# Values and keys by seven products: another order of the products, and one PSUM tile of two banks for two of them

## The chip, the cores and the metric

The kernel runs on one core of a Trainium2 chip. The metric is the time of one execution on the device, in microseconds (us), as the median of several runs. All values are float32.

## The reference

Sixteen samples of x, each 1024 nodes by 256 channels, go through two layers; only the first is touched here.

```
h   = max(layernorm(x), 0)                       # per sample, 1024 x 256
A   = 2 * | |sigmoid(difference of column means) - 0.5| - 0.5 |
g   = relu((h.T @ (adj * A)) * para)             # queries, 256 x 1024
k,v = halves of h @ kv_w                         # kv_w is 256 x 512
x   = x + softmax(q k.T * scale) v               # 4 heads of 64
# second layer, for every sample, with batch norm over all samples:
h1  = max(layernorm(x), 0)
x   = x + bn(relu(bn((A_hat @ h1) @ W1.T)) @ W2.T)
```

## The kernel before

**Order of the work.** The order of instructions on each engine is written out by hand; the program's waits are then set by the tile framework from what each instruction reads and writes. A tile is the unit of this tracking, and a tile taken from a pool waits until all readers of the tile that had its place are through. For each sample b the kernel runs `attention(b)` (scores, exponentials, weighted values), then `graph_seven(b + 1)`, which makes queries, keys and values of the next sample, then `linear1_all(b)`, the first matrix products of layer two for the sample just finished. Sample 0 and sample 1 get their keys and values from the plainer `graph`; samples 2 to 15, 14 in all, from `graph_seven`. The change lies in the second half of `graph_seven`.

**Seven products.** Keys and values are block products with 2 x 2 blocks, done by a scheme with seven products in place of eight. The class `Seven` holds one such product; `V` makes values (turned, so that nodes lie on partitions) and `K` makes keys. `product(m)` issues product m on TensorE: for `K` one matmul of 128 x 512 (line 713), for `V` four matmuls of 128 x 128 (line 718). In the profile each float32 matmul shows as two records. Products 1, 6, 5 and 3 are added up in one PSUM tile, the running sum "x"; after each of 1, 6, 5 and 3 ScalarE copies the present sum out (`copy`, line 728), and the next of them may not be added before the copy is done. Products 2, 7 and 4 have PSUM places of their own and are added by VectorE to what was copied (`add`, line 731): 2 once, 7 twice, 4 once.

**PSUM.** The kernel uses eight banks, each a place of 128 x 512 float32. The pool `ps_s` has three slots of two banks, `ps_o` and `ps_t` one bank each. `ps_s` also holds the score tiles of attention, the tiles `gps[0]` and `gps[1]` of the graph product, and the sums of `linear1` (line 1027). Before the change `product` takes a tile for itself when it needs one: both running sums, values' fourth and keys' seventh from `ps_s` (one of a slot's two banks is then used), values' seventh and keys' fourth from `ps_o`, both seconds from `ps_t`.

**What stands around it.** Just before, TensorE ends the graph product in `f_gpsx` (in `ps_t`) and `f_gps7` (in `ps_o`). ScalarE copies `f_gpsx` (line 656); VectorE adds `gps[1]` (line 658), the block sums `kt1` to `kt4` (lines 663 to 667), `f_gps7` (line 668) and `gps[0]` (line 670). Then, between the products, VectorE's queue holds, in this order: `V.add(0, 0, 2)`, two multiplications that make the queries (line 740), `add1` (line 938, which adds the attention's result to x), the statistics `norm.stats(0, 4)` and `norm.invert(0, 4)` (lines 253 to 259; GpSimd makes the power, line 260), `V.add(1, 0, 7)` and `V.add(1, 1, 7)`, a shift (line 266), `norm.stats(4, NC)` and `norm.invert(4, NC)`, and `V.add(1, 0, 4)`. `norm.relu` on ScalarE (line 281) makes h of layer two, which `linear1` multiplies; its second half, `norm.relu(4, NC)`, stands behind `K.copy(0, 1)` on ScalarE. The DMAs of the stretch (`leave`, `arrive`, `load_more`) are issued between `add1` and the statistics.

Of the kernel before, what the change touches and what calls it, by code (L numbers as in the profile page):

```python
# [10 lines left out]
F32 = mybir.dt.float32  # L11
# [6 lines left out]
P = 128  # L18
# [11 lines left out]
def fast_path(  # L30
# [141 lines left out]
    ps_o = ctx.enter_context(tc.tile_pool(name="fps_o", bufs=1, space=PSUM))  # L172
    ps_t = ctx.enter_context(tc.tile_pool(name="fps_t", bufs=1, space=PSUM))


    with ExitStack() as stage:
        ps_s = stage.enter_context(tc.tile_pool(name="fps_s", bufs=3, space=PSUM))
# [20 lines left out]
        for c in range(NC):  # L198
            if LASTING[c] is None:
                t = big.tile([P, N], F32, tag=f"adj{c}", name=f"f_adj_{c}")  # L200
            else:
                t = lasting.tile(
                    [P, N], F32, tag=LASTING[c], name=f"f_adj_{c}", bufs=4 if c < 4 else 1
                )
# [304 lines left out]
        def graph_seven(b, left, norm, load_more, last):  # L509
# [16 lines left out]
            for d in range(CC):  # L526
                t = pp.tile([P, N], F32, tag="p", name=f"f_hT_{b}_{d}")
# [38 lines left out]
            x = ps_t.tile([P, 512], F32, tag="t", name=f"f_gpsx_{b}")  # L566
# [44 lines left out]
            sums = big.tile([P, 2, 4, P], F32, tag="row", name=f"f_kvs_{b}")  # L611
# [62 lines left out]
            def relu_queries(d):  # L674

                nc.scalar.activation(qT[:, d, :], qT[:, d, :], AF.Relu, scale=-SCALE)

            class Seven:


                def __init__(self, name, n, c, turned):
                    self.name, self.n, self.c, self.turned, self.ps = name, n, c, turned, {}
                    sums, o = (ps_s, "s"), (ps_o, "o")
                    self.banks = {
                        "x": sums,
                        2: (ps_t, "t"),
                        7: o if turned else sums,
                        4: sums if turned else o,
                    }

                def place(self, key, pool, tag):
                    ps = pool.tile([P, 512], F32, tag=tag, name=f"f_{self.name}ps{key}_{b}")
                    self.ps[key] = ps.rearrange("p (n q) -> p n q", n=4) if self.turned else ps

                def product(self, m):
                    w = lambda i, k: kvw_t[:, k, ts(2 * self.n + i, P)]
                    s = lambda q: sums[:, self.n, q]
                    left, right = {
                        1: (w(0, 0), part(0, 0)),
                        2: (w(0, 1), part(1, 0)),  # L700
                        3: (s(3), part(1, 1)),
                        4: (w(1, 1), kt4),
                        5: (s(0), kt1),
                        6: (s(1), kt2),
                        7: (s(2), kt3),
                    }[m]
                    more = m in (3, 5, 6)
                    key = "x" if more or m == 1 else m
                    if not more:
                        self.place(key, *self.banks[key])  # L710
                    ps = self.ps[key]
                    if not self.turned:
                        nc.tensor.matmul(  # L713
                            ps, left, right, start=not more, stop=True, skip_group_check=more
                        )
                        return
                    for n in range(4):
                        nc.tensor.matmul(  # L718
                            ps[:, n],
                            right[:, ts(n, P)],  # L720
                            left,
                            start=not more and n == 0,
                            stop=n == 3,
                            skip_group_check=True,
                        )
# [6 lines left out]

            V = Seven("v", 1, lambda i, j: v[:, 4 * j : 4 * j + 4, ts(i, P)], True)
            K = Seven("k", 0, lambda i, j: kT[:, i, ts(j, 512)], False)
            V.product(1)
            V.copy(0, 0)
            V.product(2)
            V.add(0, 0, 2)
            for d in range(CC):
                nc.vector.tensor_mul(qT[:, d, :], both(d), qT[:, d, :])  # L740
            V.product(7)
            V.product(6)
            V.copy(1, 0)
            K.product(1)
            K.copy(0, 0)
            add1()
            leave(b - 1)
            arrive(b + 1)
            load_more(2, 3)
            norm.stats(0, 4)  # L750
            norm.invert(0, 4)
            K.product(2)
            V.product(5)
            V.copy(1, 1)
# [3 lines left out]
            if last:  # L758
                K.add(0, 0, 2)
            norm.stats(4, NC)  # L760
            norm.invert(4, NC)
            K.product(6)
            K.copy(1, 0)
            V.product(4)
            V.add(1, 0, 4)
            V.product(3)
# [7 lines left out]
            if last:  # L774
                relu_queries(1)
            else:
                norm.relu(0, 4, False)
            K.product(7)
            norm.shifts(4, NC)
            if not last:  # L780
                K.add(0, 0, 2)
            K.product(4)
            K.product(3)
            K.copy(0, 1)
# [492 lines left out]
        def leave(b):  # L1277

            nc.sync.dma_start(x1_d[b].rearrange("(c p) d -> p c d", p=P), xr[b])
# [102 lines left out]
        with tc.manual_schedule(engines={ENG.PE, ENG.Activation, ENG.DVE, ENG.Pool, ENG.SP}):  # L1382
# [73 lines left out]
            for b in range(B):  # L1456
# [43 lines left out]
                if b + 1 < B:  # L1500
                    more_loads = {}

                    def load_more(k0, k1):
                        if 0 < b < B - 2:
                            more_loads.update(load_thirds(b, k0, k1))

                    if b == 0:
                        qkv = graph(b + 1, between)
                        todo = []
                    else:  # L1510
                        qkv, todo = graph_seven(b + 1, left, norm, load_more, b + 2 == B)
                        thirds = more_loads
                    if b == 0:
                        for step in scale[4:]:
                            step()
                        thirds = make_thirds(b)
# [70 lines left out]
    with ExitStack() as stage:  # L1587
# [21 lines left out]
        with tc.manual_schedule(engines={ENG.PE, ENG.Activation, ENG.DVE, ENG.Pool, ENG.SP}):  # L1609
# [7 lines left out]
            def bank(name, pool=None):  # L1617
                return (pool or ps_z).tile([P, 512], F32, tag="z", name=name)
# [22 lines left out]
            sums = lasting.tile([P, 4, 2, P], F32, tag="w2n", name="f_w2s")  # L1641
# [820 lines left out]
```

## Time and profile before

| | us |
|---|---|
| median of 3 runs | 2370.23 |
| lowest and highest | 2370.16, 2371.90 |
| the profiled execution | 2370.03 |
| its span, first to last instruction | 2368.2 |
| TensorE's mean granted clock | 0.997 |
| VectorE's additions L731 for values, 56 in all, median of one | 0.680 |
| ScalarE's copies L728 for values, 56 in all, median of one | 0.586 |

The profile is one execution as the hardware recorded it. PE is TensorE's matmuls, PEld its weight loads, DVE VectorE, ACT ScalarE, POOL GpSimd, SP the queue that issues most DMAs. A row of the timeline gives start and duration in us, then the engine, the line, the operation and its tiles, and in brackets how long the engine had been idle and what ended that. Ends of matmuls are modelled: two matmuls in a row overlap in the records, and the time that one takes in a row of them is the distance of their starts. The 14 stretches that the change touches begin at 280.9 us for sample 2 and at 1960.6 us for sample 15.

### The profile page before, as it was taken

The numbers are of one execution on the slowest core, as the hardware profiler recorded it, in microseconds if no ns is written. First come the engines' busy times: TensorE is split into PE (matmuls) and PEld (weight loads), VectorE is DVE, ScalarE is ACT, GpSimd is POOL, SyncE is SP. The second block draws the span as 40 slices with busy tenths as digits, with TensorE's granted clock in tenths as the row PEclk, the third lists the DMA queues.
The fourth block names the chain that finished last, engine by engine and source line by source line (L and its number), as shares of the span: only waits on it lengthen the run. The fifth ranks groups of instructions, "written<-read, shape, count | busy, mean of one in ns | idle before, by whom it ended". The sixth has DMA issues, their size and how long they took to land.

```text
span 2368.2 us, 25709 instructions
## 1 busy us (share of the span) xinstructions
PE 2326.9 (98%) x8258; PEld 1032.5 (44%) x8258; DVE 1986.0 (84%) x2923; ACT 1417.5 (60%) x2057; POOL 441.9 (19%) x565
## 2 busy tenths in 40 slices
PE   8999999999999999999999999999999999999995
PEld 4444444434343434444343434344444434444444
DVE  6788989897989889897989798988989898757766
ACT  6846556574838465665648384746556575346654
POOL 2041212122221112221212221121212121100000
PEclk9999999999999999999999999999999999999998
DMA  5043343433342434334343424253353521355569
GB/s 194 11 142 98 133 142 116 157 110 116 121 142 76 169 98 156 120 127 150 109 129 133 127 80 160 89 178 98 134 142 116 158 73 54 125 214 177 174 239 378
DMA packets 167264, 323.78 MB, mean 137 GB/s; under 512 B 33616, under 2 KB 100688, under 8 KB 167120
## 3 DMA queue, kind: packets, MB, share of 16 engines
q1 hardware_dynamic: 143696, 266.44, 32.9%
q0 software_dynamic: 18816, 38.83, 6.1%
q10 hardware_dynamic: 4608, 16.78, 1.7%
q8 instruction: 67, 1.10, 0.2%
q14 instruction: 77, 0.63, 0.1%
HBM read 202.38 MB, written 100.72 MB: 128 GB/s over the span
## 4 chain that ended last, share of the span: by engine, by line
PE 94%; DVE 2%; DMA 2%; POOL 1%; issue 1%; ACT 0%; SPq 0%; DVEq 0%; ACTq 0%; POOLq 0%
PE f_s L810 19%; PE f_o L862 19%; PE f_aps L1027 16%; PE f_gps L571 8%; PE f_gpsx L571 6%; PE f_zps L1134 6%; PE f_zx L1684 4%; PE f_zm L1684 3%; PE f_vpsx L718 2%; PE f_kpsx L713 2%; PE f_vps L718 1%; PE f_kps L713 1%; PE f_gps L413 1%; PE f_outps L1902 1%; PE f_vps L459 1%
## 5 line engine op out<-in xcount | busy, mean ns | idle before, releaser
L818 ACT ACTIVATE f_p<-f_s 128x1024 f32<-128x1024 f32 x512 | 477.0, 1045 | 60.7 <-PE f_s L810 60.7
L810 PE MATMUL f_s<-f_qT,f_kT 64*128 64x512 f32 x2048 | 457.0, 596 | 0.4 <-DVE f_v L731 0.4
L862 PE MATMUL f_o<-f_p,f_v 128*64 128x512 f32 x2048 | 453.6, 595 | 0.0
L810 PEld LDWEIGHTS f_s<-f_qT,f_kT 64*128 64x128 f32 x2048 | 191.1, 185 | 263.8 <-issue 116.9
L862 PEld LDWEIGHTS f_o<-f_p,f_v 128*64 128x64 f32 x2048 | 141.4, 137 | 304.3 <-issue 265.3
L366 POOL TENSOR_TENSOR f_w<-f_w,f_adj 128x1024 f32<-128x1024 f32 x56 | 132.5, 2365 | 701.5 <-ACT f_w L365 528.7
L930 POOL DMA_DIRECT2D f_att<-f_oT x256 | 136.7, 541 | 381.5 <-DVE f_oT L913 375.1
L833 DVE TENSOR_TENSOR f_acc<-f_acc,f_p 128x1024 f32<-128x1024 f32 x128 | 155.8, 1217 | 4.6 <-ACT f_p L818 4.6
L353 ACT ACTIVATE f_w<-f_row,f_col 128x1024 f32<-128x1024 f32 x127 | 147.3, 1160 | 14.0 <-DMA f_row<-frow 11.4
L833 DVE TENSOR_TENSOR f_sums<-f_sums,f_p 128x1024 f32<-128x1024 f32 x128 | 155.7, 1216 | 0.0
L356 ACT ACTIVATE f_w<-f_w 128x1024 f32<-128x1024 f32 x127 | 134.3, 1058 | 4.0
L1027 PE MATMUL f_aps<-f_ahatT,f_hs 128*128 128x512 f32 x256 | 115.1, 592 | 0.0
L1027 PE MATMUL f_aps<-f_ahatT,f_h_b 128*128 128x512 f32 x256 | 113.7, 597 | 0.3 <-DVE f_v L731 0.2
L1027 PE MATMUL f_aps<-f_t,f_hs 128*128 128x512 f32 x256 | 112.5, 592 | 0.0
L571 PE MATMUL f_gps<-f_w,f_h_a 128*128 128x512 f32 x224 | 109.9, 593 | 0.0
L365 ACT ACTIVATE f_w<-f_w,f_now 128x1024 f32<-128x1024 f32 x56 | 64.3, 1148 | 75.0 <-DVE f_now L363 75.0
L824 DVE TENSOR_TENSOR f_acc<-f_p,f_p 128x1024 f32<-128x1024 f32 x64 | 78.0, 1218 | 32.3 <-ACT f_p L818 32.3
L281 ACT ACTIVATE f_h_a<-f_x,f_shift_a,f_rstd_a 128x256 f32<-128x256 f32 x126 | 73.9, 587 | 37.8 <-DVE f_shift_a L266 37.8
L830 DVE TENSOR_TENSOR f_sums<-f_p,f_p 128x1024 f32<-128x1024 f32 x64 | 78.1, 1221 | 21.0 <-ACT f_p L818 21.0
L370 DVE SCALAR_TENSOR_TENSOR f_w<-f_w,f_adj 128x1024 f32<-128x1024 f32 x71 | 88.0, 1257 | 7.7 <-ACT f_w L356 7.7
L1157 ACT ACTIVATE f_z<-f_zps,f_b 128x512 f32<-128x512 f32 x60 | 38.0, 684 | 75.2 <-PE f_zps L1134 75.2
L846 DVE STREAM_TRANSPOSE f_sums<-f_acc 128x1024 f32<-128x1024 f32 x64 | 79.7, 1245 | 1.7
(298 smaller groups left out, 3961.5 us busy)
## 6 DMA issues: line engine op xcount, KB each, us to landing
f_t<-ft SPq DMA_DIRECT2D x84, 512.0 KB, 9.8
fz<-f_z SPq DMA_DIRECT2D x64, 512.0 KB, 9.9
f_x<-in_x_dram SPq DMA_DIRECT2D x31, 1024.0 KB, 6.0
f_zb<-fz SPq DMA_DIRECT2D x42, 512.0 KB, 4.4
fx<-f_x SPq DMA_DIRECT2D x16, 1024.0 KB, 4.4
fgs<-f_gs POOLq DMA_DIRECT2D x28, 512.0 KB, 3.0
fhT<-f_hQ POOLq DMA_DIRECT2D x112, 128.0 KB, 3.2
f_hT<-fhT SPq DMA_DIRECT2D x28, 512.0 KB, 6.5
```

Of the source, the lines that this page charges most:

```text
L353: nc.scalar.activation(w, rows[b], AF.Abs, bias=cols[b][:, c : c + 1], scale=0.5 / C)
L356: nc.scalar.activation(w, w, AF.Tanh)
L366: nc.gpsimd.tensor_mul(w, w, adj_t[c])
L571: nc.tensor.matmul(ps, left, right, start=fresh and n == 0, stop=(n == PAIRS - 1), skip_group_check=more,)
L810: nc.tensor.matmul(ps[:, e, :], kT[rows_e, pair, ts(m, P)], qT[rows_e, pair, ts(g, 512)], start=True, stop=True,)
L818: nc.scalar.activation(p, ps, AF.Exp)
L833: nc.vector.tensor_add(to, to, p)
L862: nc.tensor.matmul(o_of[s][e * HD : (e + 1) * HD, :], v[:, m, ts(2 * pair + e, HD)], p[:, e, :], start=(m == 0), stop=(m == NC - 1),)
L930: queue.dma_start(t[ts(j, 32), :, a].rearrange("r h c i -> r h (c i)"), oT[ts(a, 32), :, j].rearrange("r h c i -> r h (c i)"),)
L1027: nc.tensor.matmul(ps, left[:, m, :], right(m), start=not more and m == 0, stop=(m == KH - 1), skip_group_check=more,)
L1134: nc.tensor.matmul(ps[i], left[:, ts(i, P)], right, start=not more, stop=True, skip_group_check=more,)
L1684: nc.tensor.matmul(ps, left[:, m, :], right[:, m, :], start=start and m == 0, stop=(m == 1), skip_group_check=not start,)
```

## The change

The order in which TensorE gets the products goes from

`V1 V2 V7 V6 K1 K2 V5 K6 V4 V3 K5 K7 K4 K3` to `V1 K1 V2 V6 V7 K2 V5 K6 V4 V3 K5 K7 K4 K3`,

where V6 is values' sixth product, and so on. The tiles are now taken by the caller with `place`. Values' fourth and keys' seventh product become the two halves, each of one bank, of a single tile `shared` of `ps_s`; the other products stay in the pools that they were in. The running sums are both taken ahead of values' first product, so the slots that they get within `ps_s` can differ. The order of instructions on VectorE and ScalarE stays as it was. Lines behind the change have other numbers in the changed kernel: 713 becomes 702, 718 becomes 707, 728 becomes 717, 731 becomes 720, 740 becomes 737, and 1027 becomes 1029.

```diff
                     self.name, self.n, self.c, self.turned, self.ps = name, n, c, turned, {}
-                    sums, o = (ps_s, "s"), (ps_o, "o")
-                    self.banks = {
-                        "x": sums,
-                        2: (ps_t, "t"),
-                        7: o if turned else sums,
-                        4: sums if turned else o,
-                    }
-
-                def place(self, key, pool, tag):
-                    ps = pool.tile([P, 512], F32, tag=tag, name=f"f_{self.name}ps{key}_{b}")
+                def place(self, key, ps):
                     self.ps[key] = ps.rearrange("p (n q) -> p n q", n=4) if self.turned else ps
...
                     key = "x" if more or m == 1 else m
-                    if not more:
-                        self.place(key, *self.banks[key])
                     ps = self.ps[key]
...
             K = Seven("k", 0, lambda i, j: kT[:, i, ts(j, 512)], False)
+
+            def bank(pool, tag, name):
+                return pool.tile([P, 512], F32, tag=tag, name=f"f_{name}_{b}")
+
+            K.place("x", bank(ps_s, "s", "kpsx"))
+            V.place("x", bank(ps_s, "s", "vpsx"))
             V.product(1)
             V.copy(0, 0)
+            K.product(1)
+            V.place(2, bank(ps_t, "t", "vps2"))
             V.product(2)
             V.add(0, 0, 2)
             for d in range(CC):
                 nc.vector.tensor_mul(qT[:, d, :], both(d), qT[:, d, :])
-            V.product(7)
             V.product(6)
             V.copy(1, 0)
-            K.product(1)
             K.copy(0, 0)
+            V.place(7, bank(ps_o, "o", "vps7"))
+            V.product(7)
             add1()
             leave(b - 1)
             arrive(b + 1)
             load_more(2, 3)
             norm.stats(0, 4)
             norm.invert(0, 4)
+            K.place(2, bank(ps_t, "t", "kps2"))
             K.product(2)
...
             K.product(6)
             K.copy(1, 0)
+            shared = ps_s.tile([P, 2, 512], F32, tag="s", name=f"f_vkps_{b}")
+            V.place(4, shared[:, 0])
             V.product(4)
             V.add(1, 0, 4)
             V.product(3)
...
+            K.place(7, shared[:, 1])
             K.product(7)
             norm.shifts(4, NC)
             if not last:
                 K.add(0, 0, 2)
+            K.place(4, bank(ps_o, "o", "kps4"))
             K.product(4)
             K.product(3)
             K.copy(0, 1)
```

## The prediction

> **What bounds the kernel now.** I read the page first: shares, slices, the chain that ended last.
>
> ```profile
> PE 2326.9 (98%) x8258; PEld 1032.5 (44%) x8258; DVE 1986.0 (84%) x2923; ACT 1417.5 (60%) x2057; POOL 441.9 (19%) x565
> PE   8999999999999999999999999999999999999995
> PEclk9999999999999999999999999999999999999998
> PE 94%; DVE 2%; DMA 2%; POOL 1%; issue 1%; ACT 0%; SPq 0%; DVEq 0%; ACTq 0%; POOLq 0%
> ```
>
> TensorE is busy 98% of the span at full clock, and 94% of the last chain is its own. Nothing stands behind it with time to give back: an idle microsecond put between two matmuls is a microsecond at the end, unless some later wait of TensorE shrinks by it. The change touches only the stretch in which 14 samples (2 to 15) make values and keys, so next I read the timeline of sample 2's stretch, TensorE's products and VectorE's side of it. Columns: start, duration (us), engine, line, operation.
>
> ```profile
> 281.12 0.59 ACT L656 COPY f_kT<-f_gpsx 128x512 f32<-128x512 f32 x1 [4.56 <-PE f_gpsx L571]
> 281.81 1.11 PE L718 MATMUL f_vps<-f_kvw,f_hT 128*128 128x128 f32 x8
> 282.75 1.06 PE L718 MATMUL f_vps<-f_kvs,f_kt 128*128 128x128 f32 x8
> 283.60 0.68 DVE L731 TENSOR_TENSOR f_v<-f_v,f_vps 128x512 f32<-128x512 f32 x1
> 284.19 2.35 DVE L740 TENSOR_TENSOR f_qT<-f_kT,f_qT 128x1024 f32<-128x1024 f32 x2
> ...
> 289.79 1.02 PE L713 MATMUL f_kpsx<-f_hT,f_kvs 128*128 128x512 f32 x2
> 290.63 0.30 PEld L713 LDWEIGHTS f_kps<-f_kt,f_kvs 128*128 128x128 f32 x2 [0.64 <-ACT f_v L728]
> 290.65 1.10 PE L713 MATMUL f_kps<-f_kt,f_kvs 128*128 128x512 f32 x2
> 291.60 1.02 PE L713 MATMUL f_kps<-f_kt,f_kvw 128*128 128x512 f32 x2
> 292.45 1.02 PE L713 MATMUL f_kpsx<-f_hT,f_kvs 128*128 128x512 f32 x2
> 292.49 0.17 DVE L259 TENSOR_SCALAR f_var_b<-f_mv_b 128x4 f32<-128x4 f32 x1
> 292.56 0.68 DVE L731 TENSOR_TENSOR f_v<-f_v,f_vps 128x512 f32<-128x512 f32 x1
> 293.39 2.81 PE L1027 MATMUL f_aps<-f_ahatT,f_h_b 128*128 128x512 f32 x6
> ```
>
> See three things. Products follow each other without a hole: the printed durations overlap, and the time of one is the distance of starts, 0.86 us after a product of keys (284.54 to 285.40) and 0.89 after one of values (283.65 to 284.54). Keys' seventh starts at 290.65, right behind keys' fifth. And VectorE's addition of values' fourth product (the L731 at 292.56, ended 293.24) comes 1.9 us **after** that start, being queued behind norm.stats(4, NC) and norm.invert. From the L731 at 283.60 to that addition VectorE has no marked idle: it is a queue, not a wait for TensorE. The starts of all 14 samples agree with these to 0.02 us; only sample 12's late addition, with what follows it, is 0.28 later.
>
> **The change part by part.** The page's run took 2370.03 us, 1.83 more than its span, and 0.20 under the median of the runs (2370.23). The sum is made on 2370.03; 0.2% (4.7 us) is about what a measurement of this kernel can tell from no change.
>
> *The shared tile.* It is the term that decides. Before, values' fourth and keys' seventh product are two tiles in two slots of ps_s. After, they are halves of one tile, and the order of the built program shows what comes of it: the first matmul of keys' seventh, which waited for ScalarE (values' copy(0, 1), long over), now waits for VectorE, and a VectorE wait at that place can only be for the one reader the shared tile has by then, V.add(1, 0, 4). It stands so in all 14 samples; sample 2's rows, before and after:
>
> ```
> L713 Matmult f_kps7_2_1986<-f_kt23_2_1893,f_kvs_2_1816 128x512 [waits Activation_49]
> L702 Matmult f_vkps_2_1968<-f_kt23_2_1893,f_kvs_2_1816 128x512 [waits DVE_49]
> ```
>
> The tile is tracked as one piece, though the second half has nothing to do with the first.
>
> Price. That addition ends at 293.24 in sample 2. It starts later after the change: keys' first product is now ahead of values' second, so values' second starts 0.89 + 0.86 after values' first, at 280.92 + 1.75 = 282.67, and ends (1.05) at 283.72. VectorE picks up a TensorE result within 0.04 (ScalarE's copy L728 at 282.01 after values' first product, ended 281.97) to 0.11 us (L657 at 276.90 after the product that ended at 276.79). So V.add(0, 0, 2) starts at 283.76 to 283.83 and not 283.60: 0.16 to 0.23 late, I take 0.20. VectorE's queue has no hole in which to win it back, so V.add(1, 0, 4) ends at 293.44. From such an end to the matmul that waits for it takes 0.15 (293.24 to the L1027 at 293.39, whose tile is the one that this addition frees). Keys' seventh starts at 293.59, keys' fourth, keys' third and the first L1027 each 0.86 later: 296.17 for 293.39, **2.78 us per sample**. Queued behind the waiting matmul are just those two products and then all of linear1; ScalarE's K.copy(0, 1) and, behind it, norm.relu(4, NC) wait for keys' third and slip by the same.
>
> Is it won back? The second half of h is needed four matmuls after the first L1027, 3.4 us on; its relu starts today 0.6 after it (294.00) and stays as far behind. The other way to win back is a TensorE stall later in the sample; matmul starts show none over 0.1 us from 293.39 until the next sample's stretch. So 13 samples give 13 × 2.78 = 36.1. In sample 15 the scores follow instead: the same addition ends at 1973.52 and the first score matmul starts at 1973.58; new start 1973.52 + 0.20 + 0.15 + 3 × 0.86 = 1976.45, 2.87 late. **Sum +39.0.**
>
> *The reordering and the swapped sums.* Before, values' second waits a little for ScalarE's copy of f_gpsx (281.12 to 281.71, duration 1.11 for 1.05), and keys' seventh, after values' copy, shows 1.10 for 1.02. Keys' first product in between covers the first: at most 0.06 per sample, and the second is replaced. Both lie ahead of a wait for VectorE, so they are worth nothing to the sum. Keys' running sum takes the slot of gps[1] and waits for VectorE's L658, over at 278.4; values' seventh, behind values' sixth, waits for L668, over at 282.43 and due at about 284.45; values' sixth waits for copy(0, 0), over at 282.60, due at 283.56. Each is free, with about a microsecond of cover. Keys' fourth now waits for values' seventh matmuls and no longer for VectorE. No instruction is added or removed and no DMA moves: SP's and POOL's queues are passed by nothing. ScalarE's order of copies is unchanged, and VectorE's too.
>
> *The new hole.* TensorE would stand still from the end of keys' fifth (289.79 − 0.06 + 1.02 = 290.75) to 293.59, 2.8 us, and the granted clock may answer that. Near the end of this run, holes of 3.87 and 3.15 us were followed by half clock:
>
> ```profile
> 2320.81 3.78 PE L1902 MATMUL f_outps<-f_ident,f_z 128*128 128x128 f32 x16 [3.87 <-ACT f_z L1882]
> 2327.74 4.46 PE L1902 MATMUL f_outps<-f_ident,f_z 128*128 128x128 f32 x24 [3.15 <-ACT f_z L1882]
> 2320.90:2324.20 3.30, 3.27 (x15) 2.87 (x16) 1.11 (x1) 0.99 (x1) 0.00 (x0) 0.50 1.02 406
> 2331.20:2334.50 3.30, 2.09 (x18) 1.62 (x16) 3.14 (x4) 1.25 (x1) 0.00 (x0) 1.00 1.02 416
> ```
>
> The last two are the table by stretch: 0.50 is the clock after the first hole, 1.00 later on. Holes up to 1.00 us there had no such answer. One at 2.8 lies between, much nearer the upper rows. If one in six is answered (an estimate: a stretch that short of activity has to fall inside one 3.4 us step of the clock, and (3.4 − 2.8) / 3.4 is 0.18), that is two or three half-clock steps of 3.4 us, each losing 1.7: 0 to 4 us, put in the range, 0 in the forecast.
>
> [...]
>
> [...]
>
> **The rivals.** *Not slower:* the halves behave as two banks, keys' seventh starts as soon as keys' fifth is through, and the small stalls go. For it: the two banks are separate and the data independent. Against it: the VectorE wait in the program. Its price is bounded by the trace: the stretch takes 12.47 us (280.92 to 293.39) for 14 products, which at 0.86 would be 12.04; 0.43 × 14 = 6 us is all that could ever be won, and the stalls named (0.06, 0.08 and 0.08 before the first L1027) make 0.2 × 14 = 3 us: 2367. It decides if V.add(1, 0, 4) ends before keys' fifth does, or if nothing waits for it.
>
> *Clock in most samples:* if the 2.8 us hole is answered every time, 14 × 1.7 = 24 more: 2433. For it, the 3.15 row; against it, that the hole is shorter than a step, so that most steps keep some activity.
>
> *VectorE catches up:* the 0.20 vanishes and only the wait stays: 14 × 2.58 = 36: 2406. It needs a hole in VectorE's queue, of which the timeline shows none.
>
> **How the numbers follow.** The wait as priced (with up to three answered holes) 0.86; VectorE catching up 0.06; clock in most samples 0.04; not slower 0.04. The likeliest gives 2370.03 + 39.0 = 2409. Its unknowns: the 0.20 could be 0 (2406); the three steps behind the wait could be 0.95 as some are today (291.60 after 290.65), 3 × 0.09 × 14 = 4 more; the clock up to 4 more. Range 2405.5 to 2415. Slower by over 0.2%: 0.86 + 0.06 + 0.04 = 0.96. The not-slower case gives 2367, within 4.7 us of today: same 0.03, and 0.01 for faster, since that would need nearly all the 6 us.
>
> **What would show it.** Right: keys' seventh with a TensorE hole of 2.8 us ahead of it, released by VectorE's addition of values' fourth product, 14 times; that addition 0.2 later relative to the stretch's start; first L1027 at 15.25 after that start (12.47 now); VectorE's, ScalarE's and POOL's busy sums unchanged. The clock: half-clock steps after the holes, or none. Wrong: keys' seventh 0.86 behind keys' fifth; or the 2.78 won back by a stall that vanishes elsewhere.

## The result, and the profile after

The changed kernel takes 2436.41 us (median of six runs, 2435.18 to 2437.17) and the kernel before 2370.71 on the same chip: a ratio of 1.0276, 95% interval 1.0263 to 1.0290, or 65.7 us more. It became slower, as forecast, but by far more than the range of 2405.5 to 2415 allowed. The page, shares and last chain first:

```profile
PE 2354.0 (97%) x8258; PEld 1043.3 (43%) x8258; DVE 1986.9 (82%) x2923; ACT 1417.6 (58%) x2057; POOL 440.9 (18%) x565
PE 89%; DVE 6%; DMA 2%; issue 1%; POOL 1%; DVEq 0%; SPq 0%; ACT 0%; ACTq 0%; POOLq 0%
```

VectorE, ScalarE and GpSimd are as busy as before to 1 us, so no work was added there. TensorE has the same 8258 records and yet is busy 27 us longer: the same matmuls ran slower somewhere. And VectorE has gone from 2% to 6% of the last chain: TensorE now waits for it. The list of waits names where (us in total, times, longest):

```profile
PEld f_vkps L702 <- DVE f_v L720: 51.3, 14, 4.2
PE f_vkps L702 <- DVE f_v L720: 39.7, 14, 3.4
```

14 times, ahead of keys' seventh product (now written to f_vkps, the shared tile), released by VectorE's addition for values. The timeline of sample 2 shows both effects one behind the other; values' first product starts at 281.30 here.

```profile
290.13 1.02 PE L702 MATMUL f_kpsx<-f_hT,f_kvs 128*128 128x512 f32 x2
293.19 0.68 DVE L720 TENSOR_TENSOR f_v<-f_v,f_vkps 128x512 f32<-128x512 f32 x1
293.93 1.53 PE L702 MATMUL f_vkps<-f_kt,f_kvs 128*128 128x512 f32 x2 [2.77 <-DVE f_v L720]
295.25 1.91 PE L702 MATMUL f_kps<-f_kt,f_kvw 128*128 128x512 f32 x2
296.96 1.51 PE L702 MATMUL f_kpsx<-f_hT,f_kvs 128*128 128x512 f32 x2
298.30 7.03 PE L1029 MATMUL f_aps<-f_ahatT,f_h_b 128*128 128x512 f32 x16
```

The addition ends at 293.87 and keys' seventh starts at 293.93, after a hole of 2.77 us. Then keys' fourth takes from 295.25 to 296.96, 1.71 us for the 0.86 of before. The table by stretch tells why. A row has the stretch and its length, then the busy time of PE, PEld, DVE, ACT and POOL (with the number of instructions), the granted clock, the share of the DMA engines and GB/s. The stretches here are 3.40 us long, each on one of the 3.413 us steps in which the clock is recorded:

```profile
291.10:294.50 3.40, 0.63 (x3) 0.34 (x3) 2.82 (x14) 2.56 (x5) 1.20 (x2) 1.00 0.37 123
294.50:297.90 3.40, 3.40 (x6) 1.34 (x5) 0.66 (x2) 0.00 (x0) 0.00 (x0) 0.50 0.00 0
297.90:301.30 3.40, 3.40 (x9) 1.49 (x8) 0.21 (x1) 2.56 (x5) 0.00 (x0) 1.00 0.00 0
690.50:693.90 3.40, 1.29 (x6) 0.46 (x5) 3.31 (x15) 2.66 (x6) 1.03 (x1) 1.00 0.73 248
693.90:697.30 3.40, 2.74 (x4) 1.19 (x5) 1.37 (x4) 0.48 (x1) 1.01 (x1) 0.50 0.00 0
697.30:700.70 3.40, 3.40 (x6) 1.33 (x5) 0.00 (x0) 0.61 (x2) 0.00 (x0) 0.50 0.00 0
```

A step in which TensorE was busy for 0.63 of 3.40 us is followed by a step at half clock, in which it is fully busy and does half as much (1.71 us for one product, as above). In sample 5 (lower three rows) the step was busy for 1.29, still followed by half clock, and that one, with 0.66 us idle, by a second. All 14 holes were answered, three of them with two steps, 17 in all. That is 17 × 3.41 = 58 us at half clock; less the 3.4 us of hole that lie within these steps, half of the rest is lost (1.71 us for 0.86): 27.3 us.

So the two parts of the 65.7 us are a wait of about 38 and a slow clock of about 27. That is an account of one trace; the experiments take each part away alone.

### The profile page after: what moved, and what is told of

Same layout as the page of the kernel before. It is cut to its first block, busy times and chain, and to the rows that moved or that the text cites. A ratio compares the mean times of both kernels' runs of the same rounds, so it can differ in the third digit from the quotient of the medians.

```text
span 2433.9 us, 25724 instructions
## 1 busy us (share of the span) xinstructions
PE 2354.0 (97%) x8258; PEld 1043.3 (43%) x8258; DVE 1986.9 (82%) x2923; ACT 1417.6 (58%) x2057; POOL 440.9 (18%) x565
## 4 chain that ended last, share of the span: by engine, by line
PE 89%; DVE 6%; DMA 2%; issue 1%; POOL 1%; DVEq 0%; SPq 0%; ACT 0%; ACTq 0%; POOLq 0%
PE f_s L812 19%; PE f_o L864 18%; PE f_aps L1029 16%; PE f_gps L571 8%; PE f_gpsx L571 6%; PE f_zps L1136 6%; PE f_zx L1686 4%; PE f_zm L1686 3%; DVE f_st_b L253 2%; PE f_kpsx L702 1%; DVE f_v L720 1%; PE f_vkps L702 1%; PE f_kps L702 1%; PE f_gps L413 1%; DVE f_qT L737 1%
## 5 line engine op out<-in xcount | busy, mean ns | idle before, releaser
L717 ACT COPY f_kT<-f_kpsx 128x512 f32<-128x512 f32 x56 | 32.8, 586 | 84.4 <-PE f_kpsx L702 77.3
```

## The experiments

The theory after the result: (1) the wait on the tracked-as-one shared tile makes a hole of 2.8 us in each of 14 samples; (2) TensorE's clock answers the hole with half speed. Rivals: the new order of products and slots costs the time; a tile of two banks is itself slow; the half clock only goes along with something else.

**e1_own_tiles** gives both products tiles of their own and keeps all else of the change.

```diff
-            shared = ps_s.tile([P, 2, 512], F32, tag="s", name=f"f_vkps_{b}")
-            V.place(4, shared[:, 0])
+            V.place(4, bank(ps_s, "s", "vps4"))
...
-            K.place(7, shared[:, 1])
+            K.place(7, bank(ps_s, "s", "kps7"))
```

> The changed kernel with values' fourth and keys' seventh product in tiles of their own; order of products and order of the running sums as changed. Theory (the wait on the shared tile makes the hole, and half-clock steps of TensorE follow the hole): no hole ahead of keys' seventh, no half-clock step between 15 and 2300 us, about 2373 us; the small rest (+0.15 to 0.25 us per sample) because linear1's first matmul now waits for the addition of values' fourth, which ends 0.24 later than before. Rival A (the new order of products or the slots of the running sums cost the time): stays above 2400 us. Rival B (the order alone is a gain): 2367 to 2369 us.

Measured: 2373.22 us, ratio 1.0012 (1.0003 to 1.0021), no half-clock step between 16 and 2300 us. TensorE's timeline:

```profile
290.41 1.10 PE L702 MATMUL f_kps<-f_kt,f_kvs 128*128 128x512 f32 x2
291.36 1.02 PE L702 MATMUL f_kps<-f_kt,f_kvw 128*128 128x512 f32 x2
292.21 1.02 PE L702 MATMUL f_kpsx<-f_hT,f_kvs 128*128 128x512 f32 x2
293.44 1.95 PE L1028 MATMUL f_aps<-f_ahatT,f_h_b 128*128 128x512 f32 x4 [0.21 <-DVE f_v L720]
```

The hole is gone and with it 63 of the 66 us. What is left is the 0.21 ahead of linear1: its first tile takes the slot of values' fourth, whose addition now ends 0.24 later. The new order by itself is a small loss, 0.24 × 14 = 3.4 us, not a gain. Rivals A and B fall.

**e2_shared_only** is the kernel of before with the shared tile alone.

```diff
-                    if not more:
+                    if not more and key not in self.ps:
                         self.place(key, *self.banks[key])
...
+            shared = ps_s.tile([P, 2, 512], F32, tag="s", name=f"f_vkps_{b}")
+            V.ps[4] = shared[:, 0].rearrange("p (n q) -> p n q", n=4)
+            K.ps[7] = shared[:, 1]
             V.product(4)
```

> The kernel of before, with nothing changed but that values' fourth and keys' seventh product are halves of one two-bank tile. Theory: keys' seventh starts 12.38 us after values' first (9.74 before), the hole is about 2.5 us, linear1's first matmul is 2.5 us late by the wait and about 2 us more by half-clock steps in every sample: 2425 to 2436 us. Rival A (order and running sums cost the time): 2369 to 2373 us.

Measured: 2424.78 us, ratio 1.0228 (1.0212 to 1.0243). Keys' seventh starts 12.38 us after values' first (282.01 in sample 2), behind a hole of 2.48:

```profile
294.39 1.12 PE L713 MATMUL f_vkps<-f_kt,f_kvs 128*128 128x512 f32 x2 [2.48 <-DVE f_v L731]
295.35 1.02 PE L713 MATMUL f_kps<-f_kt,f_kvw 128*128 128x512 f32 x2
```

But only 12 of the 14 holes were answered, with 13 half-clock steps: in samples 2 and 8 keys' fourth follows 0.96 behind keys' seventh, at full clock. The shared tile alone brings most of the loss, and there is a limit to be found between these holes.

**e3_filled_hole** keeps the wait and takes the hole away: three more matmuls per sample stand behind keys' fifth, into a bank that nothing else uses.

```diff
-            V.place("x", bank(ps_s, "s", "vpsx"))
+            vx = ps_s.tile([P, 2, 512], F32, tag="s", name=f"f_vpsx_{b}")
+            V.place("x", vx[:, 0])
...
+            for _ in range(3):
+                nc.tensor.matmul(
+                    vx[:, 1], kvw_t[:, 0, ts(0, P)], part(1, 1), start=True, stop=True
+                )
             K.place(7, shared[:, 1])
```

> The changed kernel with three more 128 x 512 matmuls per sample ahead of keys' seventh, into the unused second bank of values' running sum; nobody reads their result. They last 2.6 us in a wait of 2.8, so keys' seventh still starts 12.62 us after values' first. Theory: no half-clock step between 15 and 2300 us, linear1's first matmul at 15.2, 14 x 2.72 = 38 us over before: 2408 to 2410 us, so that the clock's part, about 27 us, is gone and the wait's part stays. Rival C (the clock records accompany something else, and the 27 us come from the late copies and additions behind the wait): stays at 2430 to 2437 us.

Measured: 2408.71 us, ratio 1.0160 (1.0144 to 1.0176), no half-clock step between 16 and 2300 us. In sample 2, where values' first starts at 282.20:

```profile
291.89 2.82 PE L780 MATMUL f_vpsx<-f_hT,f_kvw 128*128 128x512 f32 x6
294.82 1.13 PE L702 MATMUL f_vkps<-f_kt,f_kvs 128*128 128x512 f32 x2
295.79 1.02 PE L702 MATMUL f_kps<-f_kt,f_kvw 128*128 128x512 f32 x2
296.64 1.02 PE L702 MATMUL f_kpsx<-f_hT,f_kvs 128*128 128x512 f32 x2
297.50 1.02 PE L1034 MATMUL f_aps<-f_ahatT,f_h_b 128*128 128x512 f32 x2
```

Keys' seventh starts at the same 12.62 us after values' first as in the changed kernel, and linear1 at 15.30 for 17.00 there. 42 matmuls **more** make the kernel 27.7 us faster than the changed one. This parts the two terms: the wait costs 38.4 us (2408.71 against 2370.27), and the slow clock that follows idle time the other 27. Rival C falls.

**e4_add_early** keeps the shared tile and moves the addition that keys' seventh waits for ahead of the additions of values' seventh.

```diff
             V.copy(1, 1)
+            shared = ps_s.tile([P, 2, 512], F32, tag="s", name=f"f_vkps_{b}")
+            V.place(4, shared[:, 0])
+            K.product(6)
+            V.product(4)
+            V.add(1, 0, 4)
             V.add(1, 0, 7)
             V.add(1, 1, 7)
...
             norm.invert(4, NC)
-            K.product(6)
             K.copy(1, 0)
-            shared = ps_s.tile([P, 2, 512], F32, tag="s", name=f"f_vkps_{b}")
-            V.place(4, shared[:, 0])
-            V.product(4)
-            V.add(1, 0, 4)
```

> The changed kernel, shared tile kept, with the addition of values' fourth product moved ahead of the two additions of values' seventh in VectorE's queue. It then ends 9.45 us after values' first, before keys' seventh is due (9.69). Theory: the wait is over when it is reached, no hole, no half-clock steps, and linear1's first matmul no longer waits for that addition either: 12.3 after values' first for 12.47 before, 2367 to 2369 us. Rival D (sharing one two-bank tile is itself slow, VectorE reading one bank while TensorE writes the other): above 2390 us.

Measured: 2372.27 us, ratio 1.0008 (0.9999 to 1.0017); the samples' stretches show no half clock. The tile of two banks costs nothing when the wait is over in time: keys' seventh starts 0.86 behind keys' fifth. Rival D falls with it as a cause of the loss. (That VectorE reads one half while TensorE writes the other happens neither here nor in the changed kernel, where the addition has ended at 293.87 when keys' seventh starts at 293.93; what it would cost is not shown.) The time itself missed my expectation by 3 us:

```profile
290.98 1.29 DVE L720 TENSOR_TENSOR f_v<-f_v,f_vps 128x512 f32<-128x512 f32 x2
291.23 1.02 PE L702 MATMUL f_vkps<-f_kt,f_kvs 128*128 128x512 f32 x2
292.18 0.16 DVE L266 SCALAR_TENSOR_TENSOR f_shift_b<-f_mv_b,f_rstd_b 128x4 f32<-128x4 f32 x1
292.41 1.10 PE L702 MATMUL f_kps<-f_kt,f_kvw 128*128 128x512 f32 x2 [0.16 <-DVE f_shift_b L266]
```

Keys' fourth is 0.32 late. Its place in ps_o is that of values' seventh, whose two additions the move had pushed back to an end 10.72 us after values' first (at 292.27), when keys' fourth was due at 10.55. The profile names VectorE's next instruction as what ended the idle time, but the built program's wait is for that addition. One wait was traded for another.

**e6_own_tiles_add_early** repairs that: own tiles, and the addition right behind those of values' seventh.

```diff
             V.add(1, 0, 7)
             V.add(1, 1, 7)
+            V.place(4, bank(ps_s, "s", "vps4"))
+            K.product(6)
+            V.product(4)
+            V.add(1, 0, 4)
             norm.shifts(0, 4)
...
             norm.invert(4, NC)
-            K.product(6)
             K.copy(1, 0)
-            shared = ps_s.tile([P, 2, 512], F32, tag="s", name=f"f_vkps_{b}")
-            V.place(4, shared[:, 0])
-            V.product(4)
-            V.add(1, 0, 4)
...
-            K.place(7, shared[:, 1])
+            K.place(7, bank(ps_s, "s", "kps7"))
```

> e1_own_tiles with the addition of values' fourth product moved up in VectorE's queue, right behind the two additions of values' seventh (e4_add_early had it ahead of them, which made keys' fourth wait for their end). Theory: the addition ends 10.6 after values' first, so linear1's first matmul no longer waits for it, and keys' fourth waits for nothing: linear1 at 12.35 for 12.47 before, 14 x 0.12 = 1.7 us less than before: 2368 to 2370 us, within what a measurement can tell. Rival: norm.shifts(0, 4), queued 0.6 later, makes ScalarE's relu late for linear1: 2373 us or more.

Measured: 2368.28 us, ratio 0.9991 (0.9982 to 1.0000). Linear1 starts 12.34 after values' first (at 293.64 in sample 2, for 281.30), for 12.47 before, so the trace shows the 0.13 × 14 = 1.8 us. It is the fastest kernel here, 68 us under the changed one. Against the kernel before, the interval ends at 1, so the gain is not clear of noise.

**e7_add_second**: the same place of the addition, with the shared tile.

> The changed kernel, shared tile kept, with the same place of the addition as in e6_own_tiles_add_early. Keys' seventh waits for its end at 10.60: it starts at 10.65 for 9.69, a hole of 0.9 to 1.0 us. Theory: the wait is paid, 12.47 goes to 13.23, 14 x 0.76 = 10.6 us, and the clock does not answer: 2380 to 2382 us. Rival E (any such hole is answered): 2390 us or more.

Measured: 2381.38 us, ratio 1.0048 (1.0032 to 1.0063), no half-clock step in the samples. Here is the wait alone at another size; values' first starts at 281.93:

```profile
290.76 1.02 PE L702 MATMUL f_kpsx<-f_hT,f_kvs 128*128 128x512 f32 x2
292.59 1.12 PE L702 MATMUL f_vkps<-f_kt,f_kvs 128*128 128x512 f32 x2 [0.81 <-DVE f_v L720]
295.27 1.02 PE L1029 MATMUL f_aps<-f_ahatT,f_h_b 128*128 128x512 f32 x2
```

Linear1 at 13.33: 0.86 × 14 = 12 us, of which 11.2 came out. Three sizes of the wait on the shared tile, all without the slow clock, give these times over the kernel before: 2 us for none (e4, where another wait was put in), 11 for 0.81 (e7) and 38 for 2.77 (e3). Nearly each microsecond of it reaches the end: 14 × 0.81 is 11.3 and 14 × 2.77 is 38.8.

**e5_one_filler** and **e8_half_filler** ask what the clock answers. They are e3 with one such matmul, and with half of one (256 columns). The edit from e3 to e5:

```diff
-            for _ in range(3):
-                nc.tensor.matmul(
-                    vx[:, 1], kvw_t[:, 0, ts(0, P)], part(1, 1), start=True, stop=True
-                )
+            nc.tensor.matmul(
+                vx[:, 1], kvw_t[:, 0, ts(0, P)], part(1, 1), start=True, stop=True
+            )
```

> The changed kernel with one added matmul per sample (128 x 512, result unread) behind keys' fifth, where e3_filled_hole had three. The hole ahead of keys' seventh is then 1.9 us for 2.77, keys' seventh still 12.62 after values' first. Theory (a half-clock step follows where one 3.41 us step of the clock holds 2.0 us or more of hole, as the rows of the changed kernel and of e2_shared_only show; 1.86 was not answered): no half-clock step between 15 and 2300 us, the same 2408 to 2410 us as with three. Rival E (what counts is any hole well over 1 us, or the share of holes in the sample): 2418 us or more.

> e5_one_filler with half the filler (128 x 256): a hole of 2.3 us. Theory: keys' seventh at 12.62 as before; a half-clock step follows in those samples, and only those, in which one clock step holds 2.0 us or more of the hole; how many depends on where the steps fall: 2410 to 2433 us. Rival F (the limit is the length of the hole, not its part within one step): all 14 are answered, or none.

Measured: e5 2412.17 us, ratio 1.0175 (1.0159 to 1.0190), with 2 of 14 holes answered in the profiled run, one of them the 0.28 longer one of sample 12; e8 2423.3 us (one run), with 9 of 14. Rivals E and F fall. My expectation for e8 held (2410 to 2433, some holes answered and some not), the one for e5 did not: 2408 to 2410 was missed by 2 us, and a step with only 1.83 us idle (sample 7) was answered, where I had put the limit at 2.0. By stretch, first e5, then e8, each stretch a step of the clock and the step behind it:

```profile
687.70:691.10 3.40, 1.57 (x5) 0.62 (x4) 2.83 (x12) 2.13 (x5) 1.01 (x1) 1.00 0.21 69
691.10:694.50 3.40, 3.40 (x10) 1.49 (x9) 0.14 (x1) 1.62 (x4) 0.00 (x0) 1.00 0.00 0
950.60:954.00 3.40, 1.57 (x5) 0.45 (x4) 3.14 (x13) 2.79 (x6) 1.33 (x2) 1.00 0.50 167
954.00:957.40 3.40, 3.40 (x5) 1.33 (x6) 0.76 (x2) 0.00 (x0) 0.29 (x1) 0.50 0.00 0
```

```profile
555.70:559.10 3.40, 1.59 (x6) 0.54 (x5) 3.35 (x14) 2.87 (x6) 1.14 (x2) 1.00 0.67 226
559.10:562.50 3.40, 2.95 (x7) 1.44 (x8) 1.15 (x3) 0.34 (x2) 0.89 (x1) 1.00 0.01 4
955.10:958.50 3.40, 1.36 (x4) 0.31 (x3) 3.35 (x13) 3.11 (x6) 1.32 (x2) 1.00 0.60 205
958.50:961.90 3.40, 3.19 (x4) 1.50 (x5) 0.92 (x3) 0.04 (x1) 0.66 (x1) 0.50 0.00 0
```

In e8 two holes of the same 2.3 us end differently: one left TensorE busy for 1.59 us of a step and was not answered, the other for 1.36 and was. In e5 two steps with the same 1.57 of busy time end differently. Over the stretches of the samples in the changed kernel, e2, e5 and e8, every step with 2.02 us or more of idle time was answered (2.06 to 3.16 in the changed kernel, 14 times), of the eight with 1.83 to 1.87 one, and none below. So in these four traces the steps that were answered part from the others between 1.8 and 2.0 us idle of 3.41, taken within one step and not over the hole.

## Why the prediction was wrong

**The wait: right.** The hole comes ahead of keys' seventh, 14 times, released by the addition of values' fourth, and measured 2.77 us for 2.8 (3.06 in sample 12 and 3.38 in sample 15; the prediction named only sample 12's addition as later than the others, by 0.28, but sample 15's is later by 0.60). Its terms: the addition starts 0.24 late for 0.20, since VectorE picks up values' second product 0.11 us after its end, and the 0.04 in the prediction is a row of ScalarE; the hand-over to TensorE takes 0.05 for 0.15, which is the delay ahead of linear1 (0.14 again in e1); and the step behind keys' seventh is 0.96, not 0.86, as e3 shows at full clock. The errors largely cancel, which is luck: linear1 is 2.83 us late in e3 for 2.78 forecast. Of that, 0.08 is won back within the sample (in e3 the samples begin 131.92 us apart, before 129.17), so 2.75 × 14 = 38.5 us, 38.4 on the chip, for 39.0 forecast. The forecast of 2409 is the time of e3 (2408.71), a kernel with the wait and without the slow clock. That the small stalls are worth nothing, that the new slots of the running sums cost nothing (the 0.24 explains all that e1 lost) and that VectorE does not catch up held as well.

**The clock: wrong, and this is the step that failed.** The prediction said of the new hole "if one in six is answered", taking 0 in the forecast and up to 4 us in the range. All 14 were, and it cost 27 us. The rival "clock in most samples" priced it at 24 and gave 2433, near the measured 2436.4, but had 4% of the chance.

Two things were wrong in that step. First, it asked for the hole to lie whole in one step of the clock. The two answered holes that it went by had left their steps nearly empty (0.1 and 0.3 us busy), but that shows no need for it, no run shows one, and one row of the same trace speaks against it. TensorE's last matmul ends in the step that begins at 2355.00, after 0.72 us of work, and 2.7 us of idle time in that step were enough:

```profile
2355.00:2358.40 3.40, 0.72 (x7) 0.48 (x5) 2.10 (x2) 0.00 (x0) 0.00 (x0) 1.00 1.02 418
2358.40:2361.80 3.40, 0.00 (x0) 0.00 (x0) 0.00 (x0) 0.00 (x0) 0.00 (x0) 0.50 1.03 413
```

Between that and 1.4 us idle (unanswered) the trace of before had nothing. An estimate from the 2.0 us that e8 and e5 show: a hole of 2.77 us goes unanswered if it is split so that neither step gets 2.0, which are 1.23 us of positions in 3.41. That is 64% answered for a random position, not 17%.

Second, the positions are not random. In the trace of the changed kernel all steps lie on one grid of 3.413 us, and the samples fall into step with it. An answered hole makes the sample 133.6 us long, and the next hole comes 39 steps (133.1 us) and 0.5 us on; so the part of it in the step drifts, over samples 2 to 5, as 2.77, 2.77, 2.36, 2.08 us. The last leaves 0.69 of the hole to the following step (0.66 in the rows above, whose bounds are rounded), and a second half-clock step follows; the sample is then 135.0 us long, and the hole is back at 2.53. The split that would go unanswered is never reached. e2, with a hole of 2.48, drifts the same way but does reach it in sample 8 (1.87, not answered).

The prediction had itself shown that a hole of 3.15 us was answered, and its estimate did not follow that row. Here about 2.0 us of idle time in one step was enough (e8, the 1.36 row).

**The two halves.** The rival "not slower" had keys' seventh start as soon as keys' fifth is through. The run agrees with the prediction's reading instead: the wait in the built program is what decided, 14 times. In e1, where the two products have tiles of their own, keys' seventh starts at 290.41, 0.86 behind keys' fifth and without a wait for the addition of values' fourth (292.62 to 293.30). That two halves of one tile could be used so is not shown by any run here.

## What to carry to other kernels

Two buffers put into one tracked tile share their waits: look in the built program for what the second writer now waits for, and where that reader stands in its own queue. Where TensorE has no slack, price a new hole twice, once as the wait and once for the half-clock steps after it (38 and 27 us here), and be ready for those to repeat in every turn of a loop: the loop of the changed kernel fell into step with the clock, and all 14 holes were answered. If a hole can't be removed, matmuls that nobody needs can be cheaper than idle time (e3, 2408.71 us for 2436.41), and a dependent addition moved forward in its queue cheaper still (e7, 2381.38 us with the shared tile kept).

## What the runs showed of the hardware that was not expected

In the trace of the changed kernel TensorE's granted clock changes only at steps of one grid of 3.413 us: the half-clock steps of samples 2 to 5 begin at 294.5, 427.6, 560.8 and 693.9 us, each 39 steps apart. In the rows above, of the samples' steps that were themselves at full clock, those busy for 1.36 us or less (0.63 and 1.29 in the changed kernel, 1.36 in e8) were followed by half clock, the one busy for 1.59 (e8) by full clock, and of the two busy for 1.57 (e5) one by each. So what exactly is counted in a step stays open. In the samples of the changed kernel a half-clock step that was idle for 0.41 us or less was followed by full clock (14 times), and one that was idle for 0.69 to 0.71 by another half-clock step (3 times). As much idle time at full clock had no such answer: e7 has 0.81 us ahead of keys' seventh, and no half-clock step in the samples. So in these runs going down and coming back went with different amounts of idle time.

Near the end of e3, where TensorE does other work (line 1909, 128x128), a shorter idle time was answered than in the samples: a step with 1.70 us idle in all, made of two holes of 0.82 and 0.88 us, was followed by half clock:

```profile
2343.20:2346.60 3.40, 1.70 (x14) 1.23 (x13) 2.44 (x5) 2.29 (x3) 0.11 (x1) 1.00 0.79 258
2346.60:2350.00 3.40, 3.40 (x18) 3.33 (x17) 2.91 (x4) 2.14 (x2) 0.00 (x0) 0.50 0.81 236
```
